# A hybrid attention, mixer and spectral kernel: the first sequence gets its own chain, the selection is cut in four, and a logarithm stands behind the gates

## The chip, the cores and the metric

The kernel runs on one core of one Trainium2 chip. The metric is the device time of one execution in microseconds (us). Its engines are TensorE (PE: matrix products and transposes, PEld: its weight loads), VectorE (DVE), ScalarE (ACT), GpSimd (POOL) and SyncE (SP), which here only issues DMAs. Each engine works off its own queue in order; engines wait for one another through semaphores. TensorE has a granted clock, full or half, which the profile shows.

## The reference

The input x holds 8 sequences of 1024 tokens (32 x 32) with 128 channels, all in 32-bit floats. Two layers follow each other.

Layer 0 is attention with 4 heads of 32. x is group-normalized, and q, k and v are projected from it. q and k are divided by their lengths along the *token* axis; the scores times 10 go through a softmax; the result is projected and added:

```
x = x + conv_attn(group_norm(x))
```

Layer 1 has two parts, on layer-normalized tokens. The first is a state-space mixer (a Mamba-like block), once with "fwd" weights and once with "bwd" weights over the reversed sequence. Per direction it computes z, x, B, C and a step dt from one projection, convolves x, B and C over four tokens, applies Silu, takes dt = softplus(dt + bias) = max(v, 0) + log(1 + exp(-|v|)), runs chunks of 64 tokens with states passed from chunk to chunk, multiplies by Silu(z), normalizes and projects. The second is a spectral unit: four candidate filter banks of 16 spectral filters and a 3-tap regression, mixed by weights that a hard selection makes:

```
y_soft = softmax(log_weights + gumbel)
y_hard = one_hot(argmax(y_soft), 4)
weights = y_hard - y_soft + y_soft
```

## The kernel before

The program has one fast path in three stages. A general path behind it is entered only if the attention's denominators are out of bounds.

**Attention (0 to about 450 us).** `qkv(b)` prepares a sequence in steps (a Python generator; each `yield` ends a step): eight transposes into PSUM (L612), a copy to SBUF (L617 on ScalarE for the first sequence, otherwise on VectorE), statistics (L623, L625), two products with a group matrix, one for the mean and one for the variance (L628, L636), a reciprocal root on GpSimd (L130, L132), the normalized input (L641), q and k (L648) with their copies to SBUF (L656) and their sums of squares on ScalarE (L660), the lengths on GpSimd (L665, L667), v (L671), and the scaling of k (L684). `add_bias` (L605) adds the output bias to the residual on GpSimd.

The work proper is cut in 128 units: sequence, half of the queries, block of 128 keys. Unit n's `scores` are four products of 32 rows (L702) and two Exp on ScalarE (L707); the unit before is summed in `weigh` (L723, L732), and `total` (L743) sums the denominators. The loop over n calls everything in a fixed order, written out by hand: on TensorE, VectorE, ScalarE and GpSimd no scheduler moves an instruction. Between the units it takes one step at a time from generators, each at fixed n: `coming` (the next sequence's `qkv`), `mixing` (mixer weights, then the selection and the mixing of the filter banks, L214 to L280), `making` (the angles and sines of the transforms, L289 to L302), `going` (the filter taps). `mixing` has five calls in 16 units, 40 in all.

Transposes, scores and other products share a PSUM pool of three tiles of two banks; a new tile waits until the readers of the tile three before are done. Two more banks hold the sums "o" and "d".

Before the loop, the first sequence's ten steps and the first steps of `making` are called by hand. The transform tables need numbers from GpSimd (`counted`, L306, L308: an iota into one shared integer tile and its copy to floats), then angles on VectorE (L289: pieces; L295: added to a large constant; L297 and L298: the remainder, clamped), then the sine on ScalarE (L302). First comes `inv`, then `fwd`; the sine of `inv` runs in the opening, that of `fwd` together with those of the four `lags` tables at n = 73.

**Mixer (about 450 to 1010 us).** 16 units, 8 sequences times two directions (d = 0 forward, d = 1 backward). The loop body works on unit u, on the unit that follows and on the one before. Again everything, SyncE too, stands in the written order. What the change touches, in that order:

- `steps` (L495 to L521), in five pieces, for the next sequence, in the units with d = 0 except the last: the product for dt, v and -|v|, Exp, then u = e + 1 and Ln (L512, L514), then dt and dA. For the first sequence these pieces are called in the attention loop at n = 117, 121 and 123.
- `convolve(following, 0)`: the first tap is on ScalarE (L972), the three others on VectorE (L980). Two of them stand ahead of the gates, the third behind the states.
- `project_z` and `activate_z` (L947, L993): two products into PSUM and their Silu.
- `from_row` on GpSimd (L924), tied behind the last tap or the layer norm's shift, and its Relu (L934).
- `chunk_states` on TensorE (L1082), `pass_states` on VectorE (L1096, L1099), with two pairs of DMAs that move states to the other partitions (L1112).
- the third tap, `activate_x` (L985), `project_bc` (L1002), `activate_bc` (L1018), the taps of the second half, `outputs` (L1147).

These products write to a PSUM pool of two tiles, so `project_bc` needs the tile of the first z product, and that is free when its Silu is done.

ScalarE holds one table of functions at a time. Where the next function needs another one, the program has an ACT_TABLE_LOAD ahead of it; Exp, Ln, Silu and Sin each stand behind a load of their own here, copies, Identity, Relu and Square need none.

**Spectral unit (about 1010 to 1412 us).** Transforms, matrices per frequency, their application and the inverse transforms. The change reaches it only through `fwd`, `inv` and the mixed banks (`m_u`, `md`), which it reads.

Of the kernel before, what the change touches and what calls it, by code (L numbers as in the profile page):

```python
# [8 lines left out]
F32 = mybir.dt.float32  # L9
# [5 lines left out]
P = 128  # L15
# [30 lines left out]
def fast_kernel(ctx: ExitStack, tc: tile.TileContext, a: dict, out: bass.AP, bad: bass.AP):  # L46
# [158 lines left out]
    def select_bank(pool):  # L205
# [15 lines left out]
        nc.scalar.activation(soft, logit, AF.Exp, bias=top, accum_out=total)  # L221
        nc.vector.reciprocal(total, total)
# [7 lines left out]
        nc.vector.tensor_scalar(left, hard, -1.0, 1.0, ALU.mult, ALU.add)  # L230
        for i in range(1, NM):
            nc.vector.tensor_tensor(hard[:, i : i + 1], hard[:, i : i + 1], left[:, i - 1 : i], ALU.mult)
            nc.vector.tensor_tensor(left[:, i : i + 1], left[:, i : i + 1], left[:, i - 1 : i], ALU.mult)
        w = pool.tile([P, NM], F32, name="w")
# [47 lines left out]
    def angles(pool, dst, pieces, tag):  # L282

        for to, numbers, by in pieces:
            for i, turn in enumerate((0.25, 0.5)):
                nc.vector.tensor_scalar(to[:, :, i, :], numbers, by, turn, ALU.mult, ALU.add)  # L289
        yield  # L290

        flat = dst.rearrange("p k i m -> p (k i m)")
        w = pool.tile([P, flat.shape[-1]], F32, tag="work_w", name=f"{tag}_w")
        big = 1.5 * 2.0**23
        nc.vector.tensor_scalar(w, flat, big, None, ALU.add)  # L295
        yield
        nc.vector.scalar_tensor_tensor(flat, w, big, flat, ALU.subtract, ALU.subtract)  # L297
        nc.vector.tensor_scalar(flat, flat, 0.49999995, -0.49999995, ALU.min, ALU.max)  # L298
# [12 lines left out]
    def transforms(pool, tables):  # L311

        odd = counted(pool, [2, NF], [[512, 2], [2, NF]], 1, 0, "odd")
        place = counted(pool, [4], [[1, 4]], 0, 4, "place")
        odd_row = counted(pool, [1], [[1, 1]], 1, 2, "odd_row")
        places = counted(pool, [4, P], [[1, 4], [4, P]], 0, 0, "places")
        yield
        lag = counted(pool, [2, 2], [[-256, 2], [1, 2]], 510, -2, "lag")
        for t in (place, odd_row, lag):
            nc.vector.tensor_scalar(t, t, 1.0 / 2048.0, None, ALU.mult)  # L320
        yield from angles(pool, inv, [(inv, places, odd_row[:, 0:1])], "inv")
        yield
        yield from angles(
            pool, fwd, [(fwd[:, k : k + 1], odd[:, 0:1, :], place[:, k : k + 1]) for k in range(4)], "fwd"
        )
        yield
        for h in range(2):
            for r in range(2):
                t = pool.tile([P, 2, 2, NF], F32, name=f"lags{h}_{r}")
                for _ in angles(pool, t, [(t, odd, lag[:, h, r : r + 1])], f"lags{h}_{r}"):  # L330
                    pass
                tables.append(t)
                yield
        for t in (fwd, *tables):
            sines(t)
# [144 lines left out]
    def steps(b, seq, pd):  # L480
# [31 lines left out]
        nc.vector.tensor_scalar(u, e, 1.0, None, ALU.add)  # L512
        lg = small("sp_l")
# [77 lines left out]
    with ExitStack() as s:  # L591
# [15 lines left out]
        def qkv(b):  # L607
# [6 lines left out]

            first = b == 0
            if first:
                nc.scalar.copy(xt, pt)  # L617
            else:
                nc.vector.tensor_copy(xt, pt)
            yield  # L620
            st = p2.tile([P, 2, 6], F32, tag="st", name=f"st{b}")
            for i in range(2):
                nc.vector.bn_stats(st[:, i, :], (pt if first else xt)[:, i * 512 : (i + 1) * 512])  # L623
# [21 lines left out]
            for i, (name, dst) in enumerate((("q", qs), ("k", ks))):  # L645
# [14 lines left out]
                nc.scalar.activation(junk, pq if first else to, AF.Square, accum_out=ss[:, i : i + 1])  # L660
                if i == 0:
                    if not first:
                        add_bias(xin)
                    yield
# [16 lines left out]
            if first:  # L681
                add_bias(xin)
            yield
            nc.vector.tensor_scalar(to, to, lengths[:, 0:1], lengths[:, 1:2], ALU.mult, ALU.mult)  # L684

# [85 lines left out]
        going, making, coming = transform_taps(p1, ps_t, tables), transforms(p1, tables), qkv(0)  # L771
        s.enter_context(tc.manual_schedule(engines=IN_ORDER))

        next(making)
        for at in range(10):
            next(coming)
            for _ in range({4: 3, 5: 1, 7: 1}.get(at, 0)):
                next(making)
            if at == 4:
                sines(inv)  # L780
        next(coming, None)
        next(making)
        coming = qkv(1)
        next(coming)
        next(coming)
        for n in range(len(units) + 2):
# [33 lines left out]
            elif n == 113:  # L820
                turn_tokens(0, seqs[0], ps_t.tile([P, T], F32, tag="t", name="px0"))
            elif n == 117:
                sizes = steps(0, seqs[0], ps_t.tile([P, T], F32, tag="t", name="pd0"))
                for _ in range(3):
                    next(sizes)
            elif n in (121, 123):
                next(sizes, None)
# [10 lines left out]
    with ExitStack() as s:  # L838
# [438 lines left out]
        for at, u in enumerate(units[:-1]):  # L1277
# [46 lines left out]
            convolve(following, 0, range(pad - 1))  # L1324
# [3 lines left out]
            first_tap(following, 1)  # L1328
            for _ in normalized(b, bridge, *norm) if u.d else ():
                pass  # L1330
# [8 lines left out]
            convolve(following, 0, range(pad - 1, pad))  # L1339
# [1119 lines left out]
```

## Time and profile before

| what | value |
|---|---|
| median of three runs | 1420.11 us (1420.01 to 1421.38) |
| profiled execution | 1414.25 us, its span 1412.4 us |
| mean granted TensorE clock | 0.987 |
| TensorE busy | 1325.0 us (94%) |
| VectorE, ScalarE, GpSimd busy | 1093.9, 916.0, 530.2 us |
| first scores start | 26.78 us |
| last attention units | about 450 us |
| matrices of the spectral unit start | 1097 us |

The profile is one execution. A group's or a timeline's line reads: start, duration, engine, line of the kernel, operation, output<-inputs, shape and count, and in brackets how long the engine had been idle before and what ended that. A line of the waits reads: engine, what it was about to do, for whom it waited, total in us, number of times, the longest one.

### The profile page before, as it was taken

To read this page: it belongs to the slowest core of one execution; us is meant where nothing else is said; L and a number is where in the kernel's file an instruction comes from. 1 tells how busy PE (TensorE), PEld (TensorE's weight loads), DVE (VectorE), ACT (ScalarE), POOL (GpSimd) and SP (SyncE) were. 2 spreads that over 40 slices of the span, in tenths; PEclk is the share of its full clock that TensorE was granted. 3 is DMA by queue.
4 is the path that set the end of the run, shared out by engine and by line. 5 is a ranking of instruction groups with operands and counts; after the bars stand their busy time and mean duration, and the time that the engine had idled before them with its cause. 6 is when DMAs were issued, how large, how long until landed. Compare 5 with 4: busy or idle time off the path is not lost. (4 is left out here: it accounts for less than half of the span.)

```text
span 1412.4 us, 45313 instructions
## 1 busy us (share of the span) xinstructions
PE 1325.0 (94%) x19798; PEld 836.2 (59%) x19798; DVE 1093.9 (77%) x2141; ACT 916.0 (65%) x1423; POOL 530.2 (38%) x510
## 2 busy tenths in 40 slices
PE   5999999999999899999999999998799899999977
PEld 2323333233333466666666666665689899999964
DVE  6789888787768698978897988889644677777745
ACT  3766666766757777878787878786454555555530
POOL 2426865875610333425243434343476111111100
PEclk9999999999999999999999999999999999999999
DMA  7101111110000543434344445441459233222257
GB/s 179 46 1 31 46 38 38 38 50 27 8 1 2 124 86 77 107 77 106 82 102 91 104 92 114 89 110 42 135 189 233 76 86 81 72 78 71 71 186 299
DMA packets 139382, 123.09 MB, mean 87 GB/s; under 512 B 44808, under 2 KB 118152, under 8 KB 135080
## 3 DMA queue, kind: packets, MB, share of 16 engines
q1 hardware_dynamic: 137048, 115.93, 32.1%
q10 hardware_dynamic: 2128, 4.19, 0.8%
q8 instruction: 157, 2.57, 0.8%
q14 instruction: 49, 0.40, 0.1%
HBM read 78.15 MB, written 34.08 MB: 79 GB/s over the span
## 5 line engine op out<-in xcount | busy, mean ns | idle before, releaser
L707 ACT ACTIVATE pr<-pt 128x1024 f32<-128x1024 f32 x256 | 248.1, 1021 | 114.9 <-PE pt L702 113.5
L732 DVE TENSOR_TENSOR two<-pr,pr 128x1024 f32<-128x1024 f32 x128 | 162.3, 1308 | 19.2 <-ACT pr L707 18.7
L1525 ACT COPY gs<-pg 128x512 f32<-128x512 f32 x256 | 132.4, 603 | 64.1 <-PE pg L1512 48.3
L1523 DVE COPY gs<-pg 128x512 f32<-128x512 f32 x256 | 158.7, 683 | 14.7 <-PE pg L1512 9.7
L702 PE MATMUL pt<-q,k 32*128 32x512 f32 x1024 | 157.6, 648 | 9.4 <-ACT pr L707 4.7
L1512 PE MATMUL pg<-taps,mst 32*128 32x128 f32 x4096 | 145.6, 281 | 4.2 <-ACT gs L1525 3.4
L1512 PEld LDWEIGHTS pg<-taps,mst 32*128 32x128 f32 x4096 | 133.8, 190 | 16.2 <-issue 11.4
L723 PE MATMUL po<-pr,v 128*32 128x512 f32 x1024 | 139.7, 603 | 0.0
L938 POOL TENSOR_TENSOR ec<-ec,ct 128x2048 f32<-128x2048 f32 x16 | 83.6, 5226 | 131.8 <-ACT cums L880 69.8
L1546 PE MATMUL py<-gs,u 128*32 128x128 f32 (+1 forms) x4096 | 128.5, 277 | 1.2 <-issue 1.2
L1002 PE MATMUL pb<-bxt,wbc 128*128 128x512 f32 x256 | 115.7, 605 | 11.0 <-ACT zs L993 11.0
L980 DVE SCALAR_TENSOR_TENSOR xs<-xp,cw,xs 128x1024 f32<-128x1024 f32 x96 | 121.7, 1281 | 1.7
L1546 PEld LDWEIGHTS py<-gs,u 128*32 128x32 f32 (+1 forms) x4096 | 112.4, 141 | 8.7 <-issue 1.5
L1535 POOL TENSOR_SCALAR u<-u 128x512 f32<-128x512 f32 x16 | 23.9, 1495 | 227.8 <-DMA u<-ud 114.0
L702 PEld LDWEIGHTS pt<-q,k 32*128 32x128 f32 x1024 | 46.6, 185 | 87.2 <-issue 33.1
L1002 PEld LDWEIGHTS pb<-bxt,wbc 128*128 128x128 f32 x256 | 47.7, 191 | 69.3 <-issue 54.9
L1099 DVE SCALAR_TENSOR_TENSOR state<-state,dec,pst 128x64 f32<-128x64 f32 x448 | 87.3, 274 | 1.5 <-DVE state L1096 0.5
L1208 POOL TENSOR_TENSOR rms<-rms_v,mhalf 128x8 f32<-128x8 f32 x16 | 27.1, 1696 | 159.7 <-DVE rms_v L1206 159.7
L723 PEld LDWEIGHTS po<-pr,v 128*32 128x32 f32 x1024 | 27.6, 110 | 88.3 <-issue 84.1
L924 POOL TENSOR_TENSOR lm<-cs,lm 128x2048 f32<-128x2048 f32 x16 | 57.9, 3620 | 46.9 <-DVE xs L980 31.4
L743 PE MATMUL pd<-two,ones 128*32 128x512 f32 x512 | 73.9, 612 | 0.2
L1178 PEld LDWEIGHTS spo<-wo,y 128*128 128x128 f32 x512 | 62.2, 192 | 15.3 <-issue 10.2
(288 smaller groups left out, 2757.7 us busy)
## 6 DMA issues: line engine op xcount, KB each, us to landing
lm<-cd SPq DMA_DIRECT2D x32, 512.0 KB
ec<-cd SPq DMA_DIRECT2D x32, 512.0 KB
ud<-sp SPq DMA_DIRECT2D x8, 1024.0 KB
u<-ud SPq DMA_DIRECT2D x32, 256.0 KB
yd<-sums SPq DMA_DIRECT2D x32, 256.0 KB
moved<-state SPq DMA_DIRECT2D x48, 128.0 KB
room<-yd SPq DMA_DIRECT2D x6, 1024.0 KB
X<-in_x SPq DMA_DIRECT2D x8, 512.0 KB
```

Of the source, the lines that this page charges most:

```text
L702: nc.tensor.matmul(pt[:, i, :], lhsT=k[rows, j * P : (j + 1) * P], rhs=q[rows, cols], start=True, stop=True)
L707: nc.scalar.activation(pr[:, 2 * g : 2 * g + 2, :].rearrange("p i t -> p (i t)"), pt.rearrange("p i t -> p (i t)"), AF.Exp, scale=SCALE,)
L723: nc.tensor.matmul(po[rows, :], lhsT=vs[b][:, j, rows], rhs=pr[:, h, :], start=(j == 0), stop=(j == NT - 1))
L732: nc.vector.tensor_tensor(two, sums["pr"][:, 2 * g : 2 * g + 2, :], pr[:, 2 * g : 2 * g + 2, :], ALU.add)
L938: t = nc.gpsimd.tensor_tensor(u.ec, u.ec, u.ct.unsqueeze(1).to_broadcast([P, NH, NT, L]), ALU.mult)
L980: u.convolved = nc.vector.scalar_tensor_tensor(acc, xp[:, at : at + T], cw[u.d][:, n, i : i + 1], acc, ALU.mult, ALU.add)
L1002: nc.tensor.matmul(u.pb[:, i * 512 : (i + 1) * 512], lhsT=wbc[u.d][:, k, :], rhs=xt[:, at : at + 512], start=(k == 0), stop=(k == KC - 1),)
L1099: nc.vector.scalar_tensor_tensor(u.state[:, k, h, :], u.state[:, k - 1, h, :], u.dec[:, c, h, j : j + 1], u.pst[c][:, j, h, :], ALU.mult, ...
L1512: nc.tensor.matmul(pts[g][:, e, :], lhsT=mst[rows, n * 4 + e, :], rhs=taps[rows, cols].rearrange("p f q m i -> p (f q m i)"), start=True, ...
L1523: nc.vector.tensor_copy(to, frm)
L1525: nc.scalar.copy(to, frm)
L1546: nc.tensor.matmul(py[t * 32 : t * 32 + 32 - 16 * m, q // 2, :], lhsT=u[:, i, m:, :, :, q * FC + f].rearrange("p k b i -> p (k b i)"), rhs ...
```

## The change

*First sequence.* `qkv` loses its special cases for the first sequence, and a new function `first_qkv` takes its place, with its own order. The copy to SBUF and the statistics go by halves of 512 tokens; TensorE gets 8, 4 and 12 further transposes of the same input behind the first eight, the mean's product and the variance's product, into a tile that nobody reads; a Sin on one column is placed behind the copies; the sums of squares are taken from PSUM directly, v is copied behind them; k is not copied but scaled from PSUM into SBUF; the bias is added last. `making` is cut differently: the angles of `fwd` come first, in two portions, then those of `inv`; both sines run in the opening, `fwd` ahead of v's copy and `inv` ahead of the first Exp. `lag` moves into the later steps, and at n = 73 only the four `lags` sines are left.

*Selection.* Three `yield`s cut it in four steps. Everything that `mixing` does behind it comes three calls later.

*Mixer.* One more `yield` between u = e + 1 and the logarithm, so `steps` has six pieces. In the mixer's loop the logarithm is called behind the gates and the second half's first tap; the piece after it stays behind the states. For the first sequence u = e + 1 is called at n = 120 and the logarithm at 121. Where u is a forward unit, all three taps of the following unit's first half stand ahead of the gates, and `from_row` is tied behind the third. With the logarithm there, ScalarE has Silu load, two Silu, Identity, Ln load, Ln, two Relu, Silu load, Silu; before it had Ln load, Ln, Silu load, two Silu, Identity, two Relu, Silu.

```diff
@@ select_bank
         nc.scalar.activation(soft, logit, AF.Exp, bias=top, accum_out=total)
+        yield
         nc.vector.reciprocal(total, total)
...
         nc.vector.tensor_scalar(left, hard, -1.0, 1.0, ALU.mult, ALU.add)
+        yield
         for i in range(1, NM):
...
+        yield
         w = pool.tile([P, NM], F32, name="w")
@@ transforms
         odd = counted(pool, [2, NF], [[512, 2], [2, NF]], 1, 0, "odd")
         place = counted(pool, [4], [[1, 4]], 0, 4, "place")
+        over_2048(place)
+        by_place = [(fwd[:, k : k + 1], odd[:, 0:1, :], place[:, k : k + 1]) for k in range(4)]
+        turns(by_place[:2])
+        yield
         odd_row = counted(pool, [1], [[1, 1]], 1, 2, "odd_row")
         places = counted(pool, [4, P], [[1, 4], [4, P]], 0, 0, "places")
+        over_2048(odd_row)
+        yield
+        turns(by_place[2:])
+        yield
+        for _ in angles(pool, fwd, "fwd"):
+            yield
+        yield
+        turns([(inv, places, odd_row[:, 0:1])])
+        for _ in angles(pool, inv, "inv"):
+            yield
         yield
         lag = counted(pool, [2, 2], [[-256, 2], [1, 2]], 510, -2, "lag")
...
-        for t in (fwd, *tables):
+        for t in tables:
             sines(t)
@@ steps
         nc.vector.tensor_scalar(u, e, 1.0, None, ALU.add)
+        yield
         lg = small("sp_l")
         nc.scalar.activation(lg, u, AF.Ln)
@@ first_qkv
+            for j in range(NT):
+                nc.tensor.transpose(pt[:, j * P : (j + 1) * P], xin[:, j, :], ident)
+            busy = ps_o.tile([P, 512], F32, tag="d", name="busy")
+            def keep_busy(n):
+                for i in range(n):
+                    nc.tensor.transpose(busy[:, (i % 4) * P : (i % 4 + 1) * P], xin[:, i % NT, :], ident)
+            keep_busy(8)
...
+            for i in range(2):
+                nc.vector.bn_stats(st[:, i, :], pt[:, halves[i]])
+                nc.scalar.copy(xt[:, halves[1 - i]], pt[:, halves[1 - i]])
+            nc.scalar.activation(soon, mhalf, AF.Sin)
...
+            next(making)
+            pm = ps_t.tile([P, 1], F32, tag="t", name="pm0")
+            nc.tensor.matmul(pm, lhsT=group, rhs=mv[:, 0:1], start=True, stop=True)
+            keep_busy(4)
...
+            next(making)
+            pv = ps_t.tile([P, 1], F32, tag="t", name="pv0")
+            nc.tensor.matmul(pv, lhsT=group, rhs=dm, start=True, stop=True)
+            keep_busy(12)
...
+            next(making)
+            nc.vector.tensor_scalar(xt, xt, mean, rstd, ALU.subtract, ALU.mult)
+            next(making)
...
+                nc.scalar.activation(junk, pq, AF.Square, accum_out=ss[:, i : i + 1])
...
+            sines(fwd)
+            v = keepq.tile([P, NT, P], F32, tag="v", name="v0")
+            nc.scalar.copy(v.rearrange("p j d -> p (j d)"), pvl.rearrange("p j d -> p (j d)"))
+            next(making)
+            nc.vector.tensor_copy(q, ps[0])
+            next(making)
+            sines(inv)
+            nc.vector.tensor_scalar(k, ps[1], lengths[:, 0:1], lengths[:, 1:2], ALU.mult, ALU.mult)
+            add_bias(xin)
@@ attention loop
-            elif n in (121, 123):
+            elif n in (120, 121, 123):
                 next(sizes, None)
@@ mixer loop
-            convolve(following, 0, range(pad - 1))
+            soon = pad - u.d
+            convolve(following, 0, range(soon))
             for n in range(2):
                 project_z(u, n)
                 activate_z(u, n)
             first_tap(following, 1)
+            next(going, None)
...
-            convolve(following, 0, range(pad - 1, pad))
+            convolve(following, 0, range(soon, pad))
```

## The prediction

> **What bounds the kernel now.** I read the busy shares first, then TensorE's waits by stage, then the timeline at each wait that the change touches, and last the granted clock.
>
> ```profile
> PE 1325.0 (94%) x19798; PEld 836.2 (59%) x19798; DVE 1093.9 (77%) x2141; ACT 916.0 (65%) x1423; POOL 530.2 (38%) x510
> ```
>
> TensorE is busy for 94%, so an edit pays only where TensorE stands still or runs at half clock. What it waits for in the attention stage (26 to 480 us; total, times, longest):
>
> ```profile
> PE pt L702 <- ACT pr L707: 4.7, 4, 3.0
> PE pt L702 <- DVE k L684: 3.9, 1, 3.9
> PE py L427 <- DVE av L763: 2.4, 1, 2.4
> PE pt L702 <- DVE xnt L619: 0.8, 1, 0.8
> ```
>
> The reader sees four places: the first scores wait 3.9 for the scaled k, the second 0.8 for the next sequence's copy, a projection waits 2.4 behind VectorE's selection, and scores wait 3.0 behind the sines at 270 us. In the mixer (560 to 960 us, all engines):
>
> ```profile
> ACT xs L985 <- DVE xs L980: 18.0, 6, 3.3
> DVE state L1096 <- PE pst L1082: 10.7, 6, 2.1
> PE pb L1002 <- ACT zs L993: 9.2, 12, 1.3
> ```
>
> TensorE's one large wait there is for the gate's Silu; ScalarE and VectorE each have one idle stretch per forward unit. The opening's timeline:
>
> ```profile
> 8.09 1.30 DVE L623 BATCH_NORM_STATS2 st<-xt 128x6 f32<-128x512 f32 x2 [0.73 <-ACT xnt L617]
> 12.79 0.81 DVE L641 TENSOR_SCALAR xnt<-xnt,mean,gn 128x1024 f32<-128x1024 f32 x1 [0.97 <-POOL gn L132]
> 13.70 3.75 PE L648 MATMUL pq<-xnt,wqkv 128*128 128x512 f32 x4 [2.08 <-issue]
> 23.75 2.34 POOL L605 TENSOR_TENSOR X<-X,bout 128x1024 f32<-128x1024 f32 x1
> 23.82 2.82 DVE L684 TENSOR_SCALAR k<-k,inv 128x1024 f32<-128x1024 f32 x1 [1.77 <-POOL inv L667]
> 26.78 2.09 PE L702 MATMUL pt<-q,k 32*128 32x512 f32 x8 [3.94 <-DVE k L684]
> ```
>
> pq's four rows take 3.75; the same four at 265.44 take 1.98, so the opening runs at half clock. The k scale takes 2.82 instead of its median 0.76, because GpSimd's bias addition began 0.06 before it. The clock in stretches (columns: stretch, sum, five engines' busy time, clock, DMA):
>
> ```profile
> 22.80:26.10 3.30, 0.04 (x1) 0.00 (x0) 2.29 (x1) 2.04 (x2) 3.21 (x3) 1.00 0.48 115
> 26.30:29.60 3.30, 2.09 (x8) 0.54 (x8) 3.27 (x4) 0.70 (x1) 0.00 (x0) 0.50 0.16 4
> 1026.30:1029.60 3.30, 3.30 (x13) 2.94 (x12) 0.00 (x0) 0.00 (x0) 2.74 (x6) 0.50 0.46 135
> 1029.80:1031.00 1.20, 1.20 (x7) 1.07 (x6) 0.00 (x0) 0.30 (x1) 0.00 (x0) 1.00 1.00 290
> ```
>
> An idle stretch ahead of the first scores is followed by half clock; a stretch filled by eight transposes and a few matmuls gives the full clock back.
>
> **The change part by part.** The sum is made on the profiled execution (1414.25 us, its span 1412.4 and 1.85 around it), which lies 5.86 under the median 1420.11; the gain is taken off the median.
>
> *Opening, up to the normalized input.* The two copies and two statistics by halves look parallel, but in the built program each waits for the one before: statistics 0.65, copy 0.60 (the row of gs, 128x512), statistics 0.65, 0.06 for each hand-over, then 0.21: 7.02 + 2.2 = 9.3 against 9.62 before. It is lost again: odd_row's cast now stands behind the statistics, places' iota on GpSimd (0.56) waits for that cast, and the mean waits behind the second cast (0.43) and a 0.15 scaling: about 10.8, was 10.37. Four fwd turns (0.206 each, 0.82) stand ahead of the variance copy: 12.2, was 11.65. The normalized input ends at about 14.2, was 13.60. On TensorE pm stands behind 8 unread transposes (0.24 each cold, done at 8.95, before the statistics), pv behind 4 (done before dm), pq behind 12: 1.4 at full clock (0.114 each, the row at 21.80), done before the input; 2.9 cold, 0.7 too late.
>
> *From there to k.* Before, 13.04 passed from that input's end to k's (26.64). VectorE now runs, in pitches of the old rows: fwd 1.26 and 0.75, inv turns 0.92, 0.72, q copy 1.14, inv 1.26 and 0.75, k straight from PSUM 1.22 (the row of the k copy): 8.0 to 8.3. ScalarE and GpSimd reach the lengths earlier: pq and pk at full clock 3.5, then 2.21 from junkk's start to the bias addition's start: 5.8. That addition (2.34) begins some 0.3 before the last inv clamp and can block it as it blocked k: clamp at 8.7, k at 9.9. So k ends between 22.5 and 24.1, a gain of 2.5 to 4.1; I take 3.2, the two being about as likely. The cold transposes give 2.5 also: q's copy then waits for pq, and k for the lengths at about 8.8. The fwd sine ahead of v's copy and the inv sine ahead of the first Exp (1.06 each) fit under k (1.22) and the scores. The next sequence's copy now follows k at once (two fwd rows, 1.9, are gone from between): the 0.8 wait goes. Opening: 4.0. TensorE still idles 2.2 to 3.8 ahead of the first scores, so I leave the half clock after it as it was; without it the first scores and products (2.09, 2.37, 1.55, later 1.14, 1.14, 1.07) would give 2.7 more. Ends: 2.5 (the 0.8 comes back elsewhere) and 4.1 + 0.8 + 2.7 = 7.6.
>
> A rule that speaks against the unread transposes: the Trainium skill, "TensorE: Matmul & The Clock Gate", Part 4, says that transposes do not count as busy for the clock. The row 1026.30 speaks against it: 1.65 of its 3.30 are the end of eight transposes (1025.98 to 1027.95), and the clock rose, while 2.09 of 3.30 at 26.30 did not raise it. By the rule the opening would gain 3.3, by the row 4.0.
>
> *Selection.* Its VectorE operations run in one piece from 98.8 to 103.5 and push the av product to 105.3; TensorE waits 2.38. In pieces of at most 1.7, units apart, that wait goes, but the same work stays on a VectorE that is 90% busy between 100 and 200, and 0.95 of it now precedes the next den copy. Worth 2.0; ends 0.5 and 2.4. All later mixing on GpSimd and its loads and stores on SP move three calls later (32nd of 40 calls becomes the 35th): the last md store is issued by about 390, its reader is at 1021; m_u's reader is later still. The lengths of the last sequence then queue behind one mixing (7 operations, some 6 us), as earlier sequences' did. Cost nothing. The lag pieces add 0.31 to VectorE at 55 us, where it is 76% busy: nothing.
>
> *Sines at 270.* The five sines and two table loads take 5.8 of ScalarE; fwd's 1.06 leaves. TensorE's 2.98 becomes 1.9. If that also spares the half clock behind it (2.41, 1.93, 1.50 against 1.14, 1.07, 1.06) it is 2.6 more. I take 1.1; ends 1.0 and 3.6.
>
> *Mixer.* The step u in six forward units; I show the one at 690.
>
> ```profile
> 688.48 1.28 ACT L514 ACT_TABLE_LOAD   x1
> 690.05 1.28 ACT L993 ACT_TABLE_LOAD   x1
> 691.34 1.94 ACT L993 ACTIVATE zs<-pz 128x1024 f32<-128x1024 f32 x2
> 692.42 7.14 PE L1002 MATMUL pb<-bxt,wbc 128*128 128x512 f32 x16 [1.19 <-ACT zs L993]
> 699.61 1.06 ACT L985 ACTIVATE xs<-xs 128x1024 f32<-128x1024 f32 x1 [3.31 <-DVE xs L980]
> ```
>
> Without the logarithm ahead, the Silu's load runs at 688.48 and the first gate ends at 690.8; TensorE's states end at 691.23, so the 1.19 to 1.29 goes in each of six units: 7.2. Late next would be the moved states' transfer, issued until 698.7 and wanted at 701.4 instead of 702.6. Behind the gates stand the logarithm's load 1.28, its 0.26, and one more Silu load 1.28, seven times in all. Queued behind them: Relu, which starts at 694.5, was 694.3, and xs's Silu, which may start at 697.8 where it started at 699.61; the idle 3.31 takes the load. If that cover were gone, 1.28 a unit. The third tap (1.28) moves ahead of the states into VectorE's idle 2.11, and the xs chain behind the states ends as much earlier, so VectorE keeps pace with TensorE. GpSimd's lm (3.62) waits for that tap and ends at 694.2, just before Relu wants it. I take 6.8; ends 3.6 (half comes back in the next wait) and 7.3.
>
> The skill's "ScalarE: Activation LUTs", What ACT_TABLE_LOAD costs, adds about 1.38 of drain to each switch. Here the logarithm starts 0.01 after its load's end, so 1.28 is the whole; with 2.66 the idle 3.31 would still cover the load.
>
> Also in the attention, u = e + 1 moves one unit ahead of its logarithm: TensorE's wait there was 0.39, counted as nothing.
>
> Sum: 4.0 + 2.0 + 1.1 + 6.8 = 13.9, so 1420.1 - 13.9 = 1406.2.
>
> **The rivals.** *Clock held:* TensorE stays at full clock through the first units. For it: the idle ahead of the scores shrinks. Against: 2.2 to 3.8 is still most of a window. 2.7 more: 1403.5.
>
> *Opening gives nothing:* cold transposes, GpSimd first, the wait for k merely handed on. For it: the serial halves and the later mean. Without the 4.0: 1410.2.
>
> *Mixer's wait comes back:* pb starts earlier but the outputs wait for the moved states or xs, leaving 1 of 6.8: 1412. For it: VectorE is 82 to 87% busy between 600 and 900. Against it: the transfer's last issue ends 2.7 before the outputs' second half wants it.
>
> *Nothing adds up:* also opening and selection come back as VectorE's later waits, 2 in all: 1418.
>
> *Slower:* the extra Silu load lands on the path. It decides when ScalarE's idle ahead of xs in a forward unit is under 1.28; then seven times 1.28 = 9.0 is added and the 6.8 is not gained: 1420.1 - 7.1 + 9.0 = 1422. Against it: the idle is 18.0 over six units.
>
> **How the numbers follow.** Chances: forecast 0.45, clock held 0.14, opening nothing 0.11, mixer back 0.14, nothing adds up 0.05, slower 0.11. A difference under 0.2% (2.8 us) can't be told from none here: faster 0.84, same 0.05, slower 0.11. All upper ends together give 20.9, 1399; all lower ends 7.6, 1412.5, which takes in the rivals down to the mixer's return. Range 1399 to 1414; outside it the last two and little else.
>
> **What would show it.** Right: first scores at 22.5 to 24.5; no wait of av at 105; about 1.9 behind the sines; pb's wait under 0.2 in forward units, with xs's idle still above zero. Wrong: pk's rows at 0.85 after 14 us, the inv clamp at its 0.69 though GpSimd adds (k early), an "sy" wait on moved, or xs without idle.

## The result, and the profile after

The changed kernel takes 1408.02 us, the median of six runs (1405.38 to 1414.80), against 1420.06 for the kernel before (1419.80 to 1421.38): 12.0 us less, a ratio of 0.9925 with a 95% interval of 0.9906 to 0.9943. The forecast was 1406.2, range 1399 to 1414. Its profiled execution took 1408.0 us (span 1406.3) and lies at its median, while the profiled execution of before lies 5.9 under its own. So the two traces differ by only 6.1 us, and a gain read from them is to be held against 6.1, not against 12.0.

Where the gain comes from, and where it goes, is read from matched instructions: the start of the same ScalarE instruction in the trace of before, minus its start in the trace of after.

| place | gain so far |
|---|---|
| fifth unit (35 us) | 3.75 |
| behind the selection (123 us) | 7.26 |
| before the sines (261 us) | 4.36 |
| behind them (290 us) | 5.31 |
| mixer, 498 us | 5.54 |
| mixer, 967 us | 10.28 |
| matrices, 1163 us | 11.00 |
| matrices, 1294 us | 8.48 |
| end | 6.1 |

Four steps up are the change's own: the opening, 3.5 at the selection, 0.95 at the sines, and 4.7 in the mixer. Three steps down were not foreseen: 2.9 between 123 and 261 us, 2.5 in the matrices of the spectral unit, whose code is the same in both kernels, and 2.4 behind them. Most of the last lies around 1360 us, where the trace of after has 10.2 us of half clock and that of before 6.8. The kernels with the mixer's part alone and the selection alone (below), which add no instruction to TensorE, lose 1.7 to 1.8 at the same place, so I do not count it as a price of the change.

The busy shares on the page after:

```profile
PE 1333.3 (95%) x19822; PEld 843.3 (60%) x19822; DVE 1094.7 (78%) x2140; ACT 925.5 (66%) x1432; POOL 534.3 (38%) x510
```

TensorE executes 24 more instructions, the unread transposes (and 24 more weight loads). TensorE's waits in the attention (22 to 476 us; total, times, longest):

```profile
PE pt L793 <- ACT pr L798: 3.7, 4, 2.0
...
PE pt L793 <- DVE k L773: 2.0, 1, 2.0
PE pd L834 <- DVE two L823: 1.7, 1, 1.7
```

The wait for k has shrunk from 3.9 to 2.0, that for the sines from 3.0 to 2.0; the selection's 2.4 is gone, and a wait of 1.7 for the pair sums is new. The opening's timeline:

```profile
13.25 0.81 DVE L738 TENSOR_SCALAR xnt<-xnt,mean,gn 128x1024 f32<-128x1024 f32 x1 [0.74 <-POOL gn L132]
14.17 1.95 PE L745 MATMUL pq<-xnt,wqkv 128*128 128x512 f32 x4
...
19.75 0.69 DVE L302 TENSOR_SCALAR inv<-inv 128x1024 f32<-128x1024 f32 x1
19.89 1.13 POOL L762 TENSOR_TENSOR inv<-ss,mhalf 128x2 f32<-128x2 f32 x1
...
21.05 1.34 DVE L773 TENSOR_SCALAR k<-pk,inv 128x1024 f32<-128x1024 f32 x1 [0.60 <-POOL inv L762]
...
22.54 4.32 PE L793 MATMUL pt<-q,k 32*128 32x512 f32 x16 [2.04 <-DVE k L773]
```

The normalized input ends at 14.06, pq's four rows take 1.95 (full clock), and the scores start at 22.54. Beside VectorE's remainder and clamp for `inv` the two small GpSimd operations for the lengths took longer than before (0.66 and 1.13, were 0.24 and 0.71), so k waited 0.60 for them. Within the 4.32 of the scores the clock falls to half again, at 24.11: the products that start before take 0.59 to 0.74 each, those behind 1.05 to 1.22. The mixer's waits (553 to 953 us):

```profile
PE sy L1228 <- issue: 6.1, 6, 1.3
...
DVE state L1177 <- PE pst L1163: 3.6, 5, 0.8
...
PE pb L1083 <- ACT zs L1074: 3.1, 7, 0.5
```

The six waits of pb of 1.2 to 1.3 in forward units are gone; the seven left are those of 0.4 to 0.5 that backward units had already. What has grown is the line "sy <- issue": TensorE stops in the middle of the output products and waits for nothing that the profile shows. In the kernel before (560 to 960 us) it read:

```profile
PE sy L1147 <- issue: 3.5, 5, 0.8
```

ScalarE no longer waits ahead of xs. In the unit at 690:

```profile
681.92 1.28 DVE L1061 SCALAR_TENSOR_TENSOR xs<-xp,cw,xs 128x1024 f32<-128x1024 f32 x1
...
689.05 1.28 ACT L1066 ACT_TABLE_LOAD   x1
690.34 1.06 ACT L1066 ACTIVATE xs<-xs 128x1024 f32<-128x1024 f32 x1
```

The last tap of xs ends at 683.20, so its Silu waits for ScalarE's own queue alone.

### The profile page after: what moved, and what is told of

Same layout as the page of the kernel before. It is cut to its first block, busy times and chain, and to the rows that moved or that the text cites. A ratio compares the mean times of both kernels' runs of the same rounds, so it can differ in the third digit from the quotient of the medians.

```text
span 1406.3 us, 45361 instructions
## 1 busy us (share of the span) xinstructions
PE 1333.3 (95%) x19822; PEld 843.3 (60%) x19822; DVE 1094.7 (78%) x2140; ACT 925.5 (66%) x1432; POOL 534.3 (38%) x510
## 5 line engine op out<-in xcount | busy, mean ns | idle before, releaser
L1629 PEld LDWEIGHTS py<-gs,u 128*16 128x16 f32 (+1 forms) x4096 | 113.7, 141 | 12.3 <-issue 3.8
```

Of the source, the lines that this page charges most:

```text
L1629: nc.tensor.matmul(py[t * 32 : t * 32 + 32 - 16 * m, q // 2, :], lhsT=u[:, i, m:, :, :, q * FC + f].rearrange("p k b i -> p (k b i)"), rhs ...
```

## The experiments

Two theories were set against each other. **The blocks:** TensorE's instructions come to it in blocks of 256 (the trace of after has 157 transfers of 16 KB on an instruction queue, for 39897 instructions of TensorE); the unread transposes shift every later block edge by 48 instructions, and where an edge falls into a run of very short products TensorE stops. **The next wait:** what the change frees is taken back by the next late producer (moved states, VectorE).

What to look at is the "output stretch": 256 products sy and 256 weight loads of one unit, 512 records (a record is one product or one weight load in the trace), 5.23 us where nothing stops. The trace of after, one stretch with a stop and one without (columns: stretch, sum, busy time of five engines, clock, DMA):

```profile
655.71:662.47 6.76, 5.46 (x258) 4.95 (x257) 4.51 (x4) 4.84 (x8) 3.09 (x1) 1.00 0.34 101
690.95:696.19 5.24, 5.24 (x258) 4.86 (x257) 4.70 (x4) 4.52 (x8) 1.38 (x1) 1.00 0.24 50
```

In the first, TensorE stood for 1.3, from 660.01 on. A transfer of 16 KB on the instruction queue ran from 659.09 to 660.05, and TensorE went on at 661.30. The moved states had landed by 656.9, three microseconds before the stop.

### The parts alone

Mixer alone:

```diff
+        yield                                # steps: between u = e + 1 and Ln
-            elif n in (121, 123):
+            elif n in (120, 121, 123):
-            convolve(following, 0, range(pad - 1))
+            soon = pad - u.d
+            convolve(following, 0, range(soon))
             first_tap(following, 1)
+            next(going, None)
-            convolve(following, 0, range(pad - 1, pad))
+            convolve(following, 0, range(soon, pad))
```

> The kernel before with the mixer's part alone (the logarithm's step behind the gates, the third tap ahead of the states, u one unit ahead in the attention). In the changed kernel the mixer gave about 5 of its 6.8 us; TensorE's stretches of output matmuls took 95.8 us there in all against 92.0 before, and stops of 0.9 to 1.4 stand inside them. Theory A, instruction blocks: TensorE's instructions arrive in blocks of 256 (39849 instructions before, 39897 after, a transfer of 16 KB each 256 on average), and the 24 unread transposes (48 instructions) shift where a block ends inside the stretch of small output matmuls. Without the opening nothing is shifted: the output stretches take 92 again, the mixer gives 8 to 9 and the time is some 1411 to 1412. Theory B, the next wait (moved states, VectorE) takes part of the gain back: the same stops as in the changed kernel, a gain of 4.5 to 5.5, 1415.

Measured: 1413.6, ratio 0.9941 (0.9922 to 0.9959). Between 498 and 967 us it gains 6.1, between the two forecasts. The stretches take 92.8 in all (before 92.0), and their stops stand at the records of the kernel before, 376 and 432. So the next wait takes nothing large back.

Opening alone (the kernel before with `first_qkv`, the new `transforms` and nothing else):

> The kernel before with the first sequence's own chain, its unread transposes and the new order of the transforms, and nothing else. Both: first scores at 22.5, gain 3.75 at the fifth unit and some 4.7 behind the sines at 265. Theory A (instruction blocks): the shift by 48 instructions makes the output stretches of the mixer take about 95.8 instead of 92, so that 3 to 4 of the 4.7 are lost between 560 and 960 us and the whole gain is 0.5 to 2. Theory B (the next wait behind the gates): the mixer is not touched, so it takes what it took, and the gain is 4 to 5.

Measured: 1414.2, ratio 0.9946 (0.9929 to 0.9964). The trace goes with the blocks: a gain of 6.2 at 261 us, then -3.0 between 498 and 967 us, in a mixer that is not touched (stretches 96.3), and another -2.3 between 1163 and 1294. The wait of av at 105 is still there (2.4). By the medians the gain is 6.7, more than 0.5 to 2: the forecast was made against the profiled execution of before, which was a short one.

Selection alone (the three `yield`s):

> The kernel before with the selection in four pieces and nothing else (mixing three calls later). The wait of 2.4 at 105 goes. If the later mixing on VectorE and GpSimd brings a new wait of TensorE near 165 (1.67 in the changed kernel, pd behind the pair sums) the gain is 0.4 to 0.8 and cannot be told from none; if that wait came from the opening's earlier start, the gain is the 2.0 of the prediction.

Measured: 1420.4, ratio 0.9988 (0.9975 to 1.0002), no difference that can be told. In the trace 3.5 are gained at the selection and 2.9 lost again by 190 us. TensorE's only wait there (90 to 200 us):

```profile
PE pd L746 <- DVE two L735: 1.7, 1, 1.7
```

The opening is the old one here, so the new wait is the selection's own doing. Added up, opening, mixer and selection alone make 1.25% (each 0.13 to 0.19 either way), the changed kernel 0.75%; opening alone had no half clock behind its first scores, and the rest of that difference is not settled.

Logarithm alone, the third tap left behind the states:

```diff
+        yield                                # steps
-            elif n in (121, 123):
+            elif n in (120, 121, 123):
             first_tap(following, 1)
+            next(going, None)
```

> The kernel before with the logarithm's step behind the gates alone; the third tap stays behind the states. With both the mixer gave 6.1 between the units at 498 and 967 us. If the tap matters (VectorE's chain behind the states is the next to be late, and the mixer's wait comes back through it): 3 to 4.5. If it is hidden anyway: 5.8 to 6.4, and the idle of ScalarE ahead of the second half of xs is longer by up to 1.28 than with both.

Measured: 1416.8, ratio 0.9986 (0.9974 to 0.9999). Between 498 and 967 us it gains 4.2 where both edits gave 6.1: the tap matters. The waits of this kernel (553 to 965 us):

```profile
ACT xs L986 <- DVE xs L981: 11.5, 7, 1.7
...
PE sx L1032 <- ACT xs L986: 2.4, 5, 0.6
```

Without the tap ScalarE still waits for VectorE's xs, and now TensorE waits for xs, which it did in this window neither before nor with both edits. By the ratios the two kernels are further apart, 0.45% or some 6 us. The trace here is the fastest of its ten runs; where the rest lies is open.

### The blocks

Without the unread transposes (the three calls of `keep_busy` taken out of the changed kernel):

> The changed kernel without its 24 unread transposes. If they raise the clock, the clock rises one window of 3.4 us or more later (13.9 becomes 17.3 or 20.7), pq and pk run at 3.7 for four rows each or part of it, and the first scores start 1.3 to 2 later. If transposes do not count for the clock, the first scores start where they did. Theory A (instruction blocks): 48 instructions less put the blocks back where they were before the change, the output stretches of the mixer take 92 instead of 95.8, and the whole is 1 to 3 faster than the changed kernel, 1405 to 1407. Theory B: the mixer stays as in the changed kernel and the whole is 1.3 to 2 slower than it, 1410.

Measured: 1406.55, ratio 0.9898 (0.9881 to 0.9914); not slower than the changed kernel. Its first scores come later and its mixer is better: the clock rises at 20.22 (13.86 with the transposes), pq takes 3.75, the scores start at 24.70 instead of 22.54; the mixer gains 6.1 instead of 4.7, and between 1163 and 1294 only 0.3 is lost instead of 2.5.

```profile
14.17 3.75 PE L742 MATMUL pq<-xnt,wqkv 128*128 128x512 f32 x4 [2.53 <-issue]
24.70 2.17 PE L790 MATMUL pt<-q,k 32*128 32x512 f32 x12 [1.20 <-DVE k L770]
```

At 35 us it is nevertheless not behind: the gain there is 4.16, against 3.75 in the changed kernel, since no half clock follows its first scores. Windows of 3.41 us on the grid on which the clock changes, changed kernel first, then without:

```profile
7.04:10.45 3.41, 2.64 (x13) 2.27 (x12) 2.05 (x7) 1.93 (x3) 0.56 (x1) 1.00 1.21 298
10.45:13.86 3.41, 3.32 (x16) 2.92 (x15) 2.60 (x11) 0.73 (x2) 1.20 (x2) 1.00 1.22 290
```

```profile
13.39:16.81 3.42, 2.64 (x3) 1.17 (x4) 3.35 (x6) 0.00 (x0) 0.00 (x0) 1.00 1.21 290
16.81:20.22 3.41, 3.41 (x5) 1.35 (x4) 1.76 (x2) 1.11 (x2) 0.00 (x0) 1.00 0.98 248
```

A window busy for 3.32, all of it unread transposes but 0.58, was followed by full clock; one busy for 2.64 was not, in either kernel. In the eight kernels with unread transposes in the opening the clock first rises between 8.3 and 16.3 us, in the six without between 16.7 and 20.2. A busy window does not always raise it at once: in the kernel without the transposes the one from 265.98 to 269.39 is busy throughout, and the clock rises at 272.80. (The column of the clock, third from the end, shows 1.00 wherever the trace has no change of the clock before; pq's 3.75 in the third row shows that it was half.)

Unread transposes of the identity in the kernel before, ahead of its first scores:

```diff
+        hold = ps_o.tile([P, 512], F32, tag="d", name="hold")
+        for i in range(24):
+            nc.tensor.transpose(hold[:, (i % 4) * P : (i % 4 + 1) * P], ident, ident)
         for n in range(len(units) + 2):
```

> The kernel before with nothing but 24 unread transposes (of the identity) ahead of the first scores, in TensorE's idle 3.94 there: 48 instructions more, as many as the changed kernel has. Clock: the idle window is filled, so TensorE stays at full clock behind the first scores, where the kernel before ran 6.8 us (13.7 in two of its variants) at half; gain at the fifth unit 2.5 to 5. Theory A (instruction blocks): from there on the kernel runs as before, but in the mixer the stops of the output stretches come 48 records earlier in a stretch (at 328 and 384 in the units at 595 and 663, where they were at 376 and 432), the stretches take 95.5 to 96.5 in all instead of 92.0, and between 1220 and 1320 us another 2 to 2.7 are lost: a whole gain of -2 to +1. Theory B (these losses come from what starts earlier in the changed opening): the 2.5 to 5 stay to the end, 1416 to 1418.

Measured: 1419.2, ratio 1.0005 (0.9994 to 1.0015). The clock was not held: the transposes ended at 24.68, k was late as ever, a second wait follows, and 10.2 us of half clock stand behind.

```profile
21.90 2.78 PE L788 MATMUL hold<-ident 128*128 128x128 f32 x24
26.90 1.15 PE L702 MATMUL pt<-q,k 32*128 32x512 f32 x8 [2.21 <-DVE k L684]
29.80 2.09 PE L702 MATMUL pt<-q,k 32*128 32x512 f32 x8 [1.75 <-DVE xnt L619]
```

The stops moved to 328 and 384, as foretold; but the stretches take 91.3, not 95.5 or more. And 2.8 were lost between 1163 and 1294, near the 2 to 2.7 foretold. So this loss needs nothing but 48 added instructions, 1100 us ahead.

The same with 18, in the changed kernel:

> The changed kernel with 18 more unread transposes (of the identity) behind the next sequence's transposes, in TensorE's idle 2.04 ahead of the first scores; 36 instructions more than the changed kernel has, 84 more than before. Clock: no half clock behind the first scores (6.8 us in the changed kernel's trace), so the gain at the fifth unit is 6.2 to 6.5 where it was 3.75, as in the opening alone, whose windows happened to fall so. Theory A (instruction blocks): the stops of the output stretches move another 36 records ahead (292 and 348 in the two units where the changed kernel has 328 and 384), and the loss of 2.1 to 2.7 between 1220 and 1320 changes: it is not the 36 that decide but where the blocks end, so the whole is 1403 to 1408. Theory B (no effect of the blocks): 2.5 to 2.7 faster than the changed kernel and the mixer and the last stage as there, 1405.4.

Measured: 1403.8, ratio 0.9895 (0.9878 to 0.9911). No half clock behind the first scores, 6.2 at the fifth unit, the second of the two stops at 348; at 292 there was none. The loss between 1163 and 1294 is 4.3.

Then the edges were to be put back to where they stood before the change, by small unread products while TensorE waits for the first sequence:

```diff
             pt = ps_t.tile([P, T], F32, tag="t", name="xt0")
+            for i in range(104):
+                h, c = i // 2 % 2 * 64, i % 2 * 64
+                nc.tensor.matmul(
+                    pt[c : c + 64, h * 8 : h * 8 + 8],
+                    lhsT=ident[h : h + 64, :64], rhs=ident[h : h + 64, :8], start=True, stop=True
+                )
```

> The changed kernel with 104 small unread matmuls (64 rows, 64x8) at the very start, where TensorE waits until 5.03 us for the first sequence: 208 instructions, so that with the 48 of the unread transposes every later instruction stands 256 after its place in the kernel before, one whole block. Theory A (instruction blocks): the stops of the output stretches stand at 376, 432 and 488 records again, as in the four kernels without a shift, the stretches take 90.5 to 93.5 in all, and the loss of 2.1 to 2.7 between 1220 and 1320 us is gone (within 0.1): 2 to 6 faster than the changed kernel, 1402 to 1406, if the small matmuls end before 5 us; each microsecond that they run longer is lost again. Theory B (the loss comes from the opening's earlier start, not from the blocks): the losses stay, 1408.

The second has 86 of them and the 18 transposes above:

> The changed kernel with 18 unread transposes ahead of the first scores and 86 small unread matmuls at the very start: 36 and 172 instructions, again one whole block with the 48. Against the kernel with the 18 alone, which lost 2.2 up to 1228 us and 2.4 between 1228 and 1294, theory A expects no loss in either stretch, stops at 376 and 432 and so 1399 to 1402; theory B 1404. Against the kernel with the small matmuls alone the first scores should not be followed by half clock, as they were not in the one kernel that had the 18: 0 to 2.7 faster.

Measured: 1416.4, ratio 0.9978 (0.9962 to 0.9995), and 1409.9, ratio 0.9928 (0.9907 to 0.9949). Both were mis-sized: each such product stands in the trace as two products and two loads, so the shifts were 464 and 428, not 256. The first sequence's transposes began at 7.18 and 6.32 instead of 5.03, the edges were in new places, and 4.7 and 3.4 were lost between 1163 and 1294. With half as many:

```diff
-            for i in range(104):
+            for i in range(52):
```

> The kernel of the last test with 52 small unread matmuls in place of 104. There each of them stood in the trace as two matmuls and two loads, so that the shift was 464 records, 208 beyond one whole block, and the stops stood at 425 and 481, and 4.7 us were lost between 1160 and 1294 us. With 52 the shift against the kernel before is 208 + 48 = 256, one whole block. They should end at about 4.4 us (104 took 5.73), before the first sequence lands, so that the opening is that of the changed kernel. Theory A (block edges): stops at 376 and 432 again, output stretches of 90.5 to 93.5 in all, nothing lost between 1160 and 1294 us (within 0.1, as in the five kernels without a shift): 1402 to 1406. Theory B (any added instruction costs there): 2 or more lost between 1228 and 1294, 1408 or more.

and 43 with the 18 transposes:

> The changed kernel with 18 unread transposes ahead of the first scores (36 records) and 43 small unread matmuls at the start (172 records): with the 48 one whole block against the kernel before. Theory A: stops at 376 and 432, nothing lost between 1160 and 1294, no half clock directly behind the first scores: 1399 to 1403, the fastest of all. Theory B: as with the 18 alone, which was 1403.8.

Measured: 1404.6, ratio 0.9902 (0.9885 to 0.9918), and 1404.1, ratio 0.9895 (0.9877 to 0.9913). With 52 what theory A foretold came: stops at 377 and 433, stretches 92.1, 0.4 lost between 1163 and 1294 us (at most 0.1 foretold). With 43 the stops came too, but 1.3 were lost there. The clock did something else than in the changed kernel: it rose at 8.3, fell at 11.7 between the short bursts of transposes and rose again at 18.6, so pq ran at half clock (3.75) in both.

All kernels by their shift, the number of TensorE's records that were added ahead of the mixer; "lost" is how far the gain falls between the two times. "Stop at" is the record of the stretch in front of which TensorE stopped, in the 4th, 6th and 8th unit (a dash: no stop of 0.1 us); the forecast is 376, 432, 488 less the shift, give or take multiples of 256.

| kernel | shift | stop at | stretches, sum of 16 | lost, 1163 to 1294 us |
|---|---|---|---|---|
| before | 0 | 376, 432, - | 92.0 | - |
| selection alone | 0 | 376, 432, 488 | 92.1 | 0.0 |
| mixer alone | 0 | 376, 432, 488 | 92.8 | 0.0 |
| logarithm alone | 0 | 376, 432, - | 90.5 | 0.1 |
| no unread transposes | 0 | 376, 432, 488 | 93.5 | 0.3 |
| 52 small products | 256 | 377, 433, 489 | 92.1 | 0.4 |
| 43 and 18 | 256 | 377, 433, 489 | 93.7 | 1.3 |
| changed kernel | 48 | 328, 384, 440 | 95.8 | 2.5 |
| opening alone | 48 | 328, 384, 440 | 96.3 | 2.3 |
| 24 in the kernel before | 48 | 328, 384, 440 | 91.3 | 2.8 |
| mixing caught up | 48 | 328, 384, 440 | 97.1 | 3.1 |
| 18 in the changed kernel | 84 | -, 348, 404 | 94.1 | 4.3 |
| 86 and 18 | 428 | 461, -, 317 | 91.8 | 3.4 |
| 104 small products | 464 | 425, 481, - | 91.3 | 4.7 |

Where a stop stands is settled by the shift, in every kernel; not every forecast place has a stop. Whether the matrices of the spectral unit lose goes with the shift too: 0 to 0.4, once 1.3, where the edges are in the old place, 2.3 to 4.7 elsewhere. How much the stretches lose is not settled: 90.5 to 93.7 where the edges are in the old place, 91.3 to 97.1 elsewhere. Three sums hold a stretch in which a stop was followed by 3.4 us of half clock, 7.8 long: mixing caught up, 18 in the changed kernel, 43 and 18.

One count settles that the stops belong to the blocks. Over the 14 kernels TensorE stops 117 times for 0.1 us or more inside an output stretch. If all of TensorE's records are numbered from the program's start, beginning with 0 and with its semaphore instructions (248 in the kernel before), 116 of the 117 stops stand in front of the same number, taken by 256: 193. In all 117, TensorE goes on 1.2 to 1.6 us after the end of the last transfer on its instruction queue. These stops add to 5.3 us in the kernel before, to 8.7 in the changed kernel, 8.5 in opening alone and 9.0 with the mixing caught up, but only to 4.9 with the 24 transposes in the kernel before; in the six other kernels with the edges in the old place it is 4.3 to 6.4.

The last column of the table by the trace, first the changed kernel, then that with 52 small products:

```profile
1162.00:1228.00 66.00, 65.98 (x2052) 60.68 (x2048) 50.14 (x113) 37.21 (x80) 8.44 (x8) 1.00 0.29 76
1228.00:1294.00 66.00, 64.83 (x1988) 58.74 (x1983) 49.05 (x107) 35.19 (x77) 8.01 (x8) 1.00 0.28 72
```

```profile
1162.00:1228.00 66.00, 66.00 (x2059) 60.83 (x2055) 50.08 (x113) 37.41 (x80) 8.27 (x8) 1.00 0.29 76
1228.00:1294.00 66.00, 66.00 (x2067) 60.96 (x2063) 50.36 (x113) 37.33 (x80) 8.24 (x8) 1.00 0.29 76
```

At the same clock the trace shows 1988 products in 66 us instead of 2067. Of the 2.5 only some 1.2 show as stops, of 0.1 to 0.3 each; the rest I could not find in the records.

### The selection's second half

The changed kernel with `or n in (23, 25, 26)` added to the calls of `mixing`, so that GpSimd's mixing is where it was:

> The changed kernel with three more calls of the mixing (behind units 23, 25 and 26), so that the selection is still in four pieces but GpSimd's mixing has caught up with the order of the kernel before. If the waits that gave the selection's gain back (0.8 near 138 and 1.7 to 1.9 at 161 to 175) come from the mixing standing three calls later, they go and the time is 2 to 2.7 less up to 260 us, with 0 to 0.7 of new wait from the pieces following each other: 1405.5 to 1407. If they come from the pieces themselves or from the earlier start, they stay and the time is that of the changed kernel.

Measured: 1405.4, ratio 0.9903 (0.9886 to 0.9919). The losses near 138 and 161 are gone (5.6 behind the selection, 5.5 at 261 us). But the selection's own gain is gone too, to 0.1 from 40 us to 261; TensorE's waits between 90 and 200 us:

```profile
PE pd L834 <- DVE two L823: 2.3, 2, 1.4
```

They stand at 109 and 111: the pieces, I take it, follow each other too closely, which no run here tests. So the later mixing was the cause of the later waits, and spreading the selection only moves a wait of VectorE's.

No version beats the changed kernel beyond doubt, and the unread transposes bring it nothing that can be told from none: the lowest median, 1403.8, has a ratio of 0.9895 (0.9878 to 0.9911) to the kernel before, and the changed kernel's interval begins at 0.9906.

## Why the prediction was right, and where not

- **Opening, 4.0: right in sum, 3.75.** The halves are serial, the mean came at 10.40 (said 10.8), the variance at 11.69 (12.2), the input at 14.06 (14.2). Of the two ways for k it took the early one: GpSimd's addition began only at 20.99, behind the clamp (0.69, ended at 20.44), and k ended at 22.39, just ahead of the range's early end of 22.5. The unread transposes were worth 2.2 in the start of the scores (22.54 against 24.70 without), but nothing at 35 us (3.75 against 4.16), where the half clock behind the scores had taken it back (with the mixing caught up, which has the transposes and no such half clock, it is 5.61). The Trainium skill's rule in "TensorE: Matmul & The Clock Gate", Part 4, that transposes do not count for the clock, is not borne out: the full clock at 13.86 followed a window of them.
- **Half clock left as before: right here, by chance.** It was 6.8 us behind the first scores in both traces. But mixer alone and selection alone run the old opening unchanged and had 13.7, and opening alone and the kernel with the mixing caught up run the new one unchanged and had none. The rival "clock held" is no other course of the kernel but another fall of the windows.
- **Selection, 2.0: wrong, 0.6.** The wait of 2.4 went as said. What failed is the sentence that all later mixing may move three calls at no cost. It runs into GpSimd and VectorE between 139 and 170 us, and TensorE waits 1.7 for the pair sums; moved back, the wait returns as 2.3.
- **Sines, 1.1: right, 0.95.** The wait went from 2.98 to 2.03, and the half clock behind it stayed.
- **Mixer, 6.8: mechanism right, size 6.1 to 7.1** where the edges are in the old place and the clock plays no part (mixer alone, no unread transposes, 52 small products), 5.2 with 43 and 18, where the clock fell once, at 858. The extra Silu load stands where it was put: in the unit at 690 the Relu ends at 689.05, the load at 690.33, and xs follows at 690.34 with no idle left. The prediction let the load be hidden in the idle of 3.31 and took "xs without idle" as a sign of being wrong; the idle is gone, and the mixer gains all the same. With the third tap moved ahead, xs has its input at 683.20, so ScalarE runs on through Relu and load without waiting for VectorE, and TensorE does not wait for xs. The sign, and the slower rival's condition, were badly chosen. In these traces the third tap is worth the 1.9 between 6.1 and 4.2.
- **Missing from the sum: the edges.** The unread transposes were priced by their place in the opening alone. In the traces, 48 instructions more cost 2.3 to 3.1 in the spectral matrices, and on average 2.7 in the output stretches (95.1 over four kernels, 92.4 over seven with the edges in the old place), though single kernels of the two groups overlap. The first is the 2.5 lost between 1163 and 1294. In the mixer the stops grew by 3.4 (8.7 against 5.3), more than the 1.4 between 4.7 and 6.1. But the same 48 in the kernel before did not lengthen them (4.9), so what decides how long a stop lasts stays open. The line of these stops, 3.5 us in 5 stops, stood in the waits of before and was not taken up.

That the forecast came within 1.8 us all the same is partly luck. In the traces the gain is 6.1 and not 13.9: 1.4 is missing at the selection, 2.1 in the mixer, 2.5 in the matrices and 2.4 behind them. This was balanced by a trace of before that lay 5.9 under its median. Two places show where it was short. Mixer alone and selection alone, in code that they share with it, are 2.2 behind it at 40 us and lose 2.3 to 2.4 more between 1000 and 1031 us; both times they have 13.7 us of half clock where the trace of before has 6.8. So the sum was made against a run with little half clock, and by the medians opening alone gained 6.7.

## What to carry to other kernels

Instructions added to a dense engine's queue have a price far behind their place: they move every later edge of its instruction blocks. Where a kernel has stretches of very short products, compare these stretches one by one before and after, and where one has grown, count TensorE's records to the stop, semaphore instructions included. And before a gain is booked for work that is cut and spread on a busy engine, look at what stands behind it in the same queue.

## What the runs showed of the hardware

**Block edges of TensorE's instructions.** Numbered from the program's start over all of TensorE's records and taken by 256, the record at which TensorE stops in an output stretch is 193 in 116 of 117 stops, with no added instructions and with every shift of the table. Waits for a producer keep their place in the code and so change their number with the shift: 88 and 176 in the kernel before are 136 and 224 in opening alone, 48 more. Counted over products and loads alone, the same edge reads 122, 110 and 98 in the 4th, 6th and 8th mixer unit (one higher in the four kernels with the small products), since the semaphore instructions between are left out. The transfers ahead of the stops take 0.9 to 1.5 us, the stops 0.1 to 1.7. The Trainium skill, "Runtime: NRT & Kernel Launch", Instruction fetch mechanics, has the blocks of 256 instructions and calls the cost of an edge mostly hidden; in stretches of 5.23 us for 512 records the stops come to 5.3 us in the kernel before and to 8.7 in the changed one.

**The clock goes by windows of 3.41 us whose place is not the program's.** Every change of the clock in a trace lies a multiple of 3.41 us from the others, and the same opening had 6.8, 10.2 or 13.7 us at half clock behind its first scores. The half clock recorded between 15 and 1400 us adds to 30.7 us in one kernel (86 and 18) and to 58.0 in another (selection alone). Part of the spread of the runs (the kernel before took 1414.8 to 1423.8 in the experiments) may come from this; beyond the two places named above it is not shown, and the mean clock of a run does not follow its time.
